# The second half of a feed-forward stage placed beside the first units of the context attention that follows it

## The chip, the cores and the metric

The kernel runs on one core of a Trainium2 chip. The metric is device time in microseconds (us) of one launch, as the median of several runs. PE is the matmul engine (TensorE), PEld its weight loads, DVE VectorE, ACT ScalarE, POOL GpSimd, and SP the engine whose queue issues nearly all DMAs here.

## The reference, cut to what matters

Two layers work on x (4 batches of 256 tokens, 256 channels) with a context of 4 batches of 4096 positions and 192 channels. Each layer is a cross attention over the context, a self-mixing attention and a feed-forward part, each added to x:

```python
x = x + _L0_xattn_ref(_layernorm(x), ctx_768, ...)
x = x + _L0_attn_ref(_layernorm(x), ...)
x = x + _L0_ffn_ref(_layernorm(x), ...)      # the stage that is moved
x = x + _L1_xattn_ref(_layernorm(x), ctx_768, ...)   # the stage it is moved beside
x = x + _L1_attn_ref(_layernorm(x), ...)
x = x + _L1_ffn_ref(_layernorm(x), ...)
```

The layer-0 feed-forward picks one of 8 experts for each token, adds the rank-4 update of that expert to the first matrix product, takes a ReLU over 1024 hidden channels, and multiplies by a second matrix:

```python
top1 = argmax(softmax(x @ gate_W.T + gate_b))
inter = relu(x @ wi_W.T + wi_b + lora[top1](x))
out = inter @ wo_W.T + wo_b
```

The layer-1 cross attention begins with scores of 4 heads of 32 channels against all 4096 positions. Only the 32 largest scores of a row are kept: `topv, topi = top_k(scores, 32)`, softmax over these, mean over the heads, then a weighted sum of context rows.

## The kernel before, in words

x stays in SBUF as 8 tiles of 128 tokens. The stages follow each other in the source (`program`, from L2040 on): layer-0 cross attention, layer-0 attention, then `l1_context_keys` (the keys of the layer-1 context attention, function `keys`, for batch 0), then `l0_ffn`, then `l1_context`, then the rest of layer 1.

`l0_ffn` (L748 to L816) normalizes all of x, turns it to channels-first (`normed_channels`, L155), works out the experts, and then runs two halves of 512 tokens. A half has 8 parts "ps_h" (L803 to L807: six matmul instructions of 512 columns on PE each, then a ReLU on ACT into `hT`) and 4 parts "ps_o" (L808 to L816: sixteen matmul instructions of 256 columns, then DVE adds the product to one tile of x, L815, and POOL adds the bias, L816). `hT` has two buffers, one for each half, and the PSUM pool of the stage has four banks.

`l1_context` (L1065) works in 32 units: 4 batches x 2 halves of the 256 tokens x 4 heads. For a unit

- `scores` (L1153) has two parts. A part is 4 mask matmuls and 4 score matmuls on PE into two PSUM tiles of two banks (pool `x1_big`, two buffers, so a part needs both), and two copies on ACT (L1175) into `sc` tiles, of which there are 8: two units.
- `best` (L1181, two parts) takes 32 MAX8 on DVE (L1187).
- `chosen` (L1189) finds the 32 largest: 4 MAX8 and 3 MATCH_REPLACE8 on DVE; POOL negates the largest (`neg`, L1198); ACT takes four exponentials of 1024 columns (L1202) into `e` tiles, of which there are 19, in a ring.
- `weighted` (L1208) cuts and weights them: four SCALAR_TENSOR_TENSOR on DVE (L1212), a reciprocal, and a diagonal matrix on POOL (L1216).

After every fourth unit, `gathered` (L1219) sums the 4 heads and multiplies by the context rows on PE (`ps_w` L1228, `ps_c` L1242, with context tiles `cx` that `load_ctx` fetches, L1143). Its steps are run one or two at a time in the following units. The loop over units (L1268) looks ahead by hand: `best(u + 1, ...)` stands around `weighted(u)`, and `scores(u + 2)` stands at the end of unit u. In units 0 to 5 of a batch the keys of the next batch are made, too (8 chunks: a DMA of 384 KB, four matmul instructions, an ACT copy, four DMAs), and its tokens are normalized and turned (`tokens`, L1109) in unit 3.

Before unit 0 stand `queries(tokens(0))`, `load_ctx(0)` (four DMAs of 768 KB and four small memsets on POOL), and the scores of units 0 and 1.

Each engine takes its instructions in a fixed order. That order is not quite the order of the source. When the program is built, a planner lists the instructions of each engine by a cost model of its own: it takes what the model has ready, and of that what stands first in the source. So in the trace the key matmuls of L1052 stand between the feed-forward's matmuls around 1535 us, although all of batch 0's keys stand ahead of the feed-forward in the source, and the layer norms of batches 1 and 2 (L95 to L99) are done around 1575 to 1592 us, although they stand in units 3 and 11. Memory comes from pools; a pool that is opened in the place of a closed one waits, tile by tile, for the last use of what lay there.

Of the kernel before, what the change touches and what calls it, by code (L numbers as in the profile page):

```python
# [11 lines left out]
F32 = mybir.dt.float32  # L12
# [7 lines left out]
PSUM = bass.MemoryType.PSUM  # L20

P = 128
B, S, D = 4, 256, 256
NB = B * 2
# [130 lines left out]
def normed_channels(c, pool, psum):  # L155

    xnT = pool.tile([P, 2, B * S], F32, tag="xnT", name="xnT")
    with c.tc.tile_pool(name="norm", bufs=1) as tmp:
        xn = tmp.tile([P, NB, D], F32, tag="xn", name="xn")
        layernorm(c, tmp, xn, c.x)  # L160
        to_channels(c, psum, xnT, xn)
    return xnT


def attn_finish(c, pool, psum, o_ps, on):
# [580 lines left out]


def l0_ffn(c, w):  # L748
    nc, tc = c.nc, c.tc
    with ExitStack() as es:  # L750
        one = es.enter_context(tc.tile_pool(name="f0_one", bufs=1))
        psum = es.enter_context(tc.tile_pool(name="f0_ps", bufs=4, space=PSUM))

        xnT = normed_channels(c, one, psum)
        two = es.enter_context(tc.tile_pool(name="f0_two", bufs=2))


# [26 lines left out]
        kept = one.tile([P, NB, 32], F32, tag="kept", name="kept")  # L784
        nc.vector.tensor_tensor(
            kept.rearrange("p n (e r) -> p (n e) r", r=4),
            low.rearrange("p n (e r) -> p (n e) r", r=4),
            hot.rearrange("p n e -> p (n e)").unsqueeze(2).to_broadcast([P, NB * 8, 4]),
            ALU.mult,
        )  # L790
        keptT = one.tile([32, B * S], F32, tag="keptT", name="keptT")
        for half in range(2):
            ps = psum.tile([P, 512], F32, tag="mm", name="ps_kt")
            for i in range(4):
                nc.tensor.transpose(ps[0:32, i * P : (i + 1) * P], kept[:, half * 4 + i, :], c.ident)
            nc.scalar.copy(keptT[:, half * 512 : (half + 1) * 512], ps[0:32, :])

        for half in range(2):
            ts = slice(half * 512, (half + 1) * 512)
            hT = two.tile([P, 8, 512], F32, tag="hT", name="hT")  # L800
            for j in range(8):
                fs = slice(j * P, (j + 1) * P)
                ps = psum.tile([P, 512], F32, tag="mm", name="ps_h")  # L803
                for k in range(2):
                    nc.tensor.matmul(ps, w.wi[:, k, fs], xnT[:, k, ts], start=(k == 0), stop=False)
                nc.tensor.matmul(ps, w.lb[:, fs], keptT[:, ts], start=False, stop=True)
                nc.scalar.activation(hT[:, j, :], ps, AF.Relu, bias=w.bi[:, j : j + 1])  # L807
# [254 lines left out]
    return w  # L1062


def l1_context(c, w, beside):  # L1065

# [11 lines left out]
    psum = w.psum  # L1078
    with ExitStack() as es:
        one = es.enter_context(tc.tile_pool(name="x1_one", bufs=1))  # L1080
        acc = es.enter_context(tc.tile_pool(name="x1_acc", bufs=1, space=PSUM))
        pst = es.enter_context(tc.tile_pool(name="x1_pt", bufs=2, space=PSUM))
        big = es.enter_context(tc.tile_pool(name="x1_big", bufs=2, space=PSUM))
        two = es.enter_context(tc.tile_pool(name="x1_two", bufs=2))
        four = es.enter_context(tc.tile_pool(name="x1_four", bufs=4))
        ews = es.enter_context(tc.tile_pool(name="x1_e", bufs=1))
        last = es.enter_context(ExitStack())
        scs = last.enter_context(tc.tile_pool(name="x1_sc", bufs=8))

        keep = one.tile([P, NB], F32, tag="keep", name="keep")  # L1090
        nc.vector.tensor_copy(keep, w.keep)
# [6 lines left out]
        places, free = [], list(tiles)  # L1098
        for u in range(len(units)):
            if u > 3:  # L1100
                g, c4 = u // 4 - 1, u % 4
# [2 lines left out]
            del free[:4]  # L1104

        def weights(u):
            return places[u]

        def tokens(b):  # L1109
# [3 lines left out]
            nc.sync.dma_start(c.xt[:, 2 * b : 2 * b + 2, :], xt)  # L1113
            xT = one.tile([P, 2, S], F32, tag="xT", name="xT")
            ps = psum.tile([P, 512], F32, tag="mm", name="ps_t")
            for k in range(2):
                for i in range(2):
                    nc.tensor.transpose(
                        ps[:, k * S + i * P : k * S + (i + 1) * P], xt[:, i, k * P : (k + 1) * P], c.ident
                    )  # L1120
            nc.vector.tensor_copy(xT.rearrange("p k n -> p (k n)"), ps)
            return xT
# [96 lines left out]
        def gathered(b, tt, es, ps_c, first, last):  # L1219

            n = 0
            for c4 in range(4):
                wTs = []
                for half in range(2):
                    ps = pst.tile([P, 512], F32, tag="pt", name="ps_w")
                    for i in range(4):
                        for h, (e, diag) in enumerate(es):
# [7 lines left out]
                    wT = two.tile([P, 512], F32, tag="wT", name="wT")  # L1235
                    nc.scalar.copy(wT, ps)  # L1236
                    wTs.append(wT)
                yield
# [11 lines left out]
                yield  # L1250
            if not last:
                return
            o = two.tile([P, DC], F32, tag="o", name="o")
# [12 lines left out]
        group, late, more = [], iter(()), iter(())  # L1266
# [1 line left out]
        for u, (b, tt, h) in enumerate(units):  # L1268
# [41 lines left out]
        last.close()  # L1310
        beside()
        for _ in late:
            pass
# [726 lines left out]
def program(tc, a, out):  # L2040
# [3 lines left out]
    with ExitStack() as es:  # L2044
# [17 lines left out]
        with tc.tile_pool(name="w_a0", bufs=1) as pool_a0:  # L2062
            pool_x0 = es.enter_context(ExitStack())
            w = l0_xattn_weights(c, pool_x0.enter_context(tc.tile_pool(name="w_x0", bufs=1, side="right")))
            pool_f0 = es.enter_context(ExitStack())
            pools, w_s4, w_f0 = [], Ctx(), Ctx()

# [8 lines left out]
            def sums(psum, last):  # L2076
# [3 lines left out]
                        pass  # L2080
                yield from s4d_sums(c, pools[0], w_s4, psum)
                pool_x0.close()
                l0_ffn_weights(c, pool_f0.enter_context(tc.tile_pool(name="w_f0", bufs=1, side="right")), w_f0)

            l0_xattn(c, w, powers)
# [2 lines left out]
        with ExitStack() as stack:  # L2088
            w = l1_context_keys(c, stack)
            for _ in w.keys(0):  # L2090
                pass
            l0_ffn(c, w_f0)
            pool_f0.close()
            w_s1 = []

            def first():
                pool = es.enter_context(tc.tile_pool(name="w_s1a", bufs=1, side="right"))
# [128 lines left out]
```

## Time and profile before

| what | value |
|---|---|
| median of 3 runs (lowest, highest) | 2508.36 us (2495.72, 2518.99) |
| the profiled execution: time, span | 2526.01 us, 2524.2 us |
| feed-forward, ps_h of the first half to its last ps_o | 1502.5 to 1550.6 us |
| feed-forward, second half | 1550.6 to 1588.4 us |
| context attention up to `chosen` of unit 0 | 1588.4 to 1604.3 us |
| units 0, 1, 2, 3 and 4 (from `neg` to the next `neg`) | 13.96, 13.60, 13.51, 13.52, 17.80 us |
| units 0 to 31 | 1604.3 to 2112 us |

The stretches are read from the timeline: the first and the last instruction of each group, and the starts of `neg` (L1198), which stands at the same place in each unit. The profiled execution took 17.65 us more than the median of the runs, so differences are worked out inside it and then set against the median. A line of the windows view gives, for a stretch of the span: its length, the busy time and the instructions of PE, PEld, DVE, ACT and POOL, the mean PE clock that was granted (1.00 is full), the share of the DMA engines' time that was used, and GB/s.

### The profile page before, as it was taken

To read this page: it belongs to the slowest core of one execution; us is meant where nothing else is said; L and a number is where in the kernel's file an instruction comes from. 1 tells how busy PE (TensorE), PEld (TensorE's weight loads), DVE (VectorE), ACT (ScalarE), POOL (GpSimd) and SP (SyncE) were. 2 spreads that over 40 slices of the span, in tenths; PEclk is the share of its full clock that TensorE was granted. 3 is DMA by queue.
4 is the path that set the end of the run, shared out by engine and by line. 5 is a ranking of instruction groups with operands and counts; after the bars stand their busy time and mean duration, and the time that the engine had idled before them with its cause. 6 is when DMAs were issued, how large, how long until landed. Compare 5 with 4: busy or idle time off the path is not lost. (4 is left out here: it accounts for less than half of the span.)

```text
span 2524.2 us, 54839 instructions
## 1 busy us (share of the span) xinstructions
PE 2379.7 (94%) x22737; PEld 1473.4 (58%) x22737; DVE 1657.5 (66%) x4026; ACT 1068.6 (42%) x1896; POOL 134.5 (5%) x208
## 2 busy tenths in 40 slices
PE   6999999999999999999999989898999999899896
PEld 4655555555555555555555544467776789456554
DVE  6666666666666666666944440898989893577554
ACT  1255555555555554556311221565656553111221
POOL 3000000000000000000000000000000010242000
PEclk7899999999999999999989999789999999798877
DMA  8221312122221222200100011310404011300110
GB/s 214 85 65 48 77 52 66 49 69 57 60 67 52 65 61 57 62 15 2 39 1 5 1 50 51 90 53 17 119 23 115 7 52 56 105 0 17 34 26 9
DMA packets 64848, 132.25 MB, mean 52 GB/s; under 512 B 12000, under 2 KB 38752, under 8 KB 64272
## 3 DMA queue, kind: packets, MB, share of 16 engines
q1 hardware_dynamic: 63088, 124.62, 17.8%
q8 instruction: 180, 2.95, 0.5%
q10 hardware_dynamic: 992, 3.02, 0.4%
q0 software_dynamic: 512, 1.05, 0.2%
q14 instruction: 76, 0.62, 0.1%
HBM read 98.14 MB, written 5.34 MB: 41 GB/s over the span
## 5 line engine op out<-in xcount | busy, mean ns | idle before, releaser
L504 DVE TENSOR_REDUCE mx<-ps_a 128x1 f32<-128x512 f32 x1024 | 659.4, 685 | 222.8 <-PE ps_a L489 219.1
L500 ACT ACTIVATE e<-ps_s 128x512 f32<-128x512 f32 x1024 | 555.8, 594 | 418.1 <-PE ps_a L489 397.8
L489 PE MATMUL ps_a<-kt,qa 32*128 32x512 f32 x2048 | 658.8, 647 | 12.2 <-DVE mx L504 9.0
L475 PE MATMUL ps_s<-qb,kt 32*128 32x256 f32 x4096 | 592.4, 401 | 0.0
L475 PEld LDWEIGHTS ps_s<-qb,kt 32*128 32x128 f32 x4096 | 349.4, 184 | 197.5 <-issue 106.7
L417 PE MATMUL o_ps<-e,v 128*32 128x256 f32 x4096 | 327.6, 391 | 0.0
L489 PEld LDWEIGHTS ps_a<-kt,qa 32*128 32x128 f32 x2048 | 231.2, 185 | 41.2 <-DVE mx L504 19.6
L1228 PEld LDWEIGHTS ps_w<-diag,e 128*128 128x128 f32 x2048 | 235.6, 194 | 24.9 <-issue 24.9
L1228 PE MATMUL ps_w<-diag,e 128*128 128x128 f32 x2048 | 241.9, 279 | 0.0
L417 PEld LDWEIGHTS o_ps<-e,v 128*32 128x32 f32 x4096 | 81.0, 108 | 246.5 <-issue 235.0
L1187 DVE MAX8 cand<-sc 128x8 f32<-128x128 f32 x1024 | 207.2, 277 | 19.5 <-ACT sc L1175 19.5
L1202 ACT ACTIVATE e<-sc,neg 128x1024 f32<-128x1024 f32 x128 | 140.7, 1143 | 119.4 <-POOL neg L1198 88.7
L1212 DVE SCALAR_TENSOR_TENSOR e<-sc,top,e 128x1024 f32<-128x1024 f32 x128 | 158.9, 1276 | 19.7 <-ACT e L1202 16.7
L1175 ACT COPY sc<-ps_s 128x1024 f32<-128x1024 f32 x128 | 123.7, 1013 | 48.7 <-PE ps_s L1166 47.4
L321 PE MATMUL ps_k<-ctxT,x_wk 32*128 32x256 f32 x1536 | 105.1, 404 | 11.6 <-DMA ctxT<-in_ctx 11.6
L1242 PEld LDWEIGHTS ps_c<-cx,wT 128*128 128x128 f32 x576 | 98.8, 196 | 21.4 <-ACT wT L1236 9.7
L1242 PE MATMUL ps_c<-cx,wT 128*128 128x193 f32 x576 | 106.4, 338 | 3.7 <-ACT wT L1236 3.7
L343 PEld LDWEIGHTS ps_v<-x_wv,ctxT 32*128 32x128 f32 x3072 | 97.5, 190 | 15.4 <-DVE mx L504 9.4
L343 PE MATMUL ps_v<-x_wv,ctxT 32*128 32x128 f32 x3072 | 104.7, 279 | 0.7
L321 PEld LDWEIGHTS ps_k<-ctxT,x_wk 32*128 32x128 f32 x1536 | 89.5, 197 | 26.4 <-issue 17.3
L1166 PE MATMUL ps_s<-kt,q 32*128 32x512 f32 x512 | 90.4, 683 | 0.0
L1052 PE MATMUL ps_k<-ctx,x_wku 96*128 96x512 f32 x128 | 71.9, 687 | 19.5 <-DMA ctx<-in_ctx 17.4
(400 smaller groups left out, 2444.9 us busy)
## 6 DMA issues: line engine op xcount, KB each, us to landing
ctxT<-in_ctx SPq DMA_DIRECT2D x62, 768.0 KB
kt<-ks SPq DMA_DIRECT2D x352, 64.0 KB
ctx<-in_ctx SPq DMA_DIRECT2D x32, 384.0 KB
cx<-in_ctx SPq DMA_DIRECT2D x16, 768.0 KB
x_w<-in_x_w SPq DMA_DIRECT2D x2, 1024.0 KB
qk<-rot SPq DMA_DIRECT2D x8, 256.0 KB
a_qk<-qk SPq DMA_DIRECT2D x16, 128.0 KB
ctxT<-in_ctx ACTq DMA_DIRECT2D x2, 768.0 KB
```

What stands on the lines that cost most here:

```text
L321: nc.tensor.matmul(ps[:, :256], w.wk[hs, gp, k, :], ctxT[hs, k, :], start=(k == 0), stop=(k == 5))
L343: nc.tensor.matmul(ps[:, ks], ctxT[hs, k, ks], w.wv[hs, gp, k, :], start=(k == 0), stop=(k == 5))
L417: nc.tensor.matmul(o_pss[u][32 * h : 32 * h + 32, :S], vs[g // 2][:, c0 : c0 + 32], ew[h][:, n % 2, :], start=(n == 0), stop=(n == GT - 1),)
L475: nc.tensor.matmul(ps[:, k * S : (k + 1) * S], kts[u % 4 // 2][hs, u % 2, ks], qbs[u][hs, :], start=True, stop=True,)
L489: nc.tensor.matmul(ps, qas[u][hs, tt * P : (tt + 1) * P], kts[u % 4 // 2][hs, u % 2, ch * 512 : (ch + 1) * 512], start=True, stop=True,)
L500: nc.scalar.activation(e, ps.rearrange("p (k n) -> p k n", k=2), AF.Exp)
L504: nc.vector.tensor_reduce(mxs[u][:, tt, h, ch : ch + 1], ps, AX.X, ALU.max)
L1187: nc.vector.max(cands[u][:, n, :], sc[u][c4][:, i // 4, (i % 4) * P : (i % 4 + 1) * P])
L1202: nc.scalar.activation(t, src, AF.Exp, bias=neg)
L1212: nc.vector.scalar_tensor_tensor(t, src, top[:, 31:32], t, ALU.is_ge, ALU.mult)
L1228: nc.tensor.matmul(ps[:, i * P : (i + 1) * P], e[c4][:, half, i * P : (i + 1) * P], diag, start=(h == 0), stop=(h == len(es) - 1),)
L1242: nc.tensor.matmul(ps_c[:, : DC + 1], wT[:, i * P : (i + 1) * P], cxs[b][t][:, j, :], start=(first and n == 0), stop=(last and n == 31),)
```

## The change

`l0_ffn` becomes a generator that stops after pairs of its first half's ps_o parts, and after each part of its second half. `l1_context` is handed that generator and runs one step of it at each place written `next(ffn)`: four times around the preparation of batch 0, after each of the four score parts of units 0 and 1, and after each score part in the loop's units 0, 1 and 2. The first step runs all up to x's tiles 0 and 1, the second finishes the first half, the third to the tenth are the second half's ps_h parts, and the last four its ps_o parts.

What goes with it, since both stages are now in memory together: `hT` has one buffer for both halves and lends its first part to the normalized x; the feed-forward's PSUM pool has three banks in place of four; the `sc` tiles lie in a pool opened earlier, on the side of the weights; 12 of the 19 `e` tiles are there from the start, and the other 7, the `cx` tiles, `wT`, `o` and the PSUM of `gathered` are opened after the feed-forward's last step, in unit 2. `load_ctx(0)` moves there too. `tokens` is split into `normed` and `turned`. `norm` as a pool of its own goes.

```diff
 def l0_ffn(c, w):
...
-        psum = es.enter_context(tc.tile_pool(name="f0_ps", bufs=4, space=PSUM))
-        xnT = normed_channels(c, one, psum)
-        two = es.enter_context(tc.tile_pool(name="f0_two", bufs=2))
+        psum = es.enter_context(tc.tile_pool(name="f0_ps", bufs=3, space=PSUM))
+        hT = one.tile([P, 8, 512], F32, tag="hT", name="hT")
+        xn = hT[:, 0:4, :].rearrange("p a (b d) -> p (a b) d", d=D)
+        layernorm(c, one, xn, c.x)
+        xnT = one.tile([P, 2, B * S], F32, tag="xnT", name="xnT")
+        to_channels(c, psum, xnT, xn)
...
         for half in range(2):
-            hT = two.tile([P, 8, 512], F32, tag="hT", name="hT")
             for j in range(8):
...
                 nc.scalar.activation(hT[:, j, :], ps, AF.Relu, bias=w.bi[:, j : j + 1])
+                if half == 1:
+                    yield
             for i in range(4):
...
                 nc.gpsimd.tensor_tensor(xi, xi, w.bo, ALU.add)
+                if half == 1 or i % 2 == 1:
+                    yield

-def l1_context(c, w, beside):
+def l1_context(c, w, scs, ffn, beside):
...
-        tiles = [ews.tile([P, 2, 512], F32, tag=f"e{i}", name=f"e{i}") for i in range(19)]
+        tiles = [ews.tile([P, 2, 512], F32, tag=f"e{i}", name=f"e{i}") for i in range(12)]
...
-        qs[0] = queries(tokens(0))
-        load_ctx(0)
+        next(ffn)
+        xt = normed(0)
+        next(ffn)
+        xT = turned(xt)
+        next(ffn)
+        qs[0] = queries(xT)
+        next(ffn)
         for u in range(2):
             for _ in scores(u):
-                pass
+                next(ffn)
...
             ahead = scores(u + 2) if u + 2 < n else iter(())
             next(ahead, None)
             next(late, None)
+            if u < 3:
+                next(ffn)
             next(ahead, None)
+            if u < 3:
+                next(ffn)
+            if u == 2:
+                for _ in ffn:
+                    pass
+                acc = es.enter_context(tc.tile_pool(name="x1_acc", bufs=1, space=PSUM))
+                pst = es.enter_context(tc.tile_pool(name="x1_pt", bufs=2, space=PSUM))
+                late_two = es.enter_context(tc.tile_pool(name="x1_late", bufs=2))
+                four = es.enter_context(tc.tile_pool(name="x1_four", bufs=4))
+                ews = es.enter_context(tc.tile_pool(name="x1_e2", bufs=1))
+                load_ctx(0)
+                tiles += [ews.tile([P, 2, 512], F32, tag=f"e{i}", name=f"e{i}") for i in range(12, 19)]
             if b + 1 < B:
...
                 if u % 8 == 3:
-                    xT = tokens(b + 1)
+                    xT = turned(normed(b + 1))
...
 def program(tc, a, out):
...
-            l0_ffn(c, w_f0)
-            pool_f0.close()
...
+            def ffn():
+                yield from l0_ffn(c, w_f0)
+                pool_f0.close()
...
-            l1_context(c, w, first)
+            l1_context(c, w, w_f0.scs, ffn(), first)
```

More of the change, by code (lines that the diff above doesn't have):

```diff
@@ L152, in to_channels @@
                 nc.vector.tensor_copy(dst, ps[:, : m * P])
[L155 to L162, printed above, removed]
 def attn_finish(c, pool, psum, o_ps, on):
@@ L1080, in l1_context @@
         one = es.enter_context(tc.tile_pool(name="x1_one", bufs=1))
-        acc = es.enter_context(tc.tile_pool(name="x1_acc", bufs=1, space=PSUM))
-        pst = es.enter_context(tc.tile_pool(name="x1_pt", bufs=2, space=PSUM))
         big = es.enter_context(tc.tile_pool(name="x1_big", bufs=2, space=PSUM))
         two = es.enter_context(tc.tile_pool(name="x1_two", bufs=2))
-        four = es.enter_context(tc.tile_pool(name="x1_four", bufs=4))
         ews = es.enter_context(tc.tile_pool(name="x1_e", bufs=1))
-        last = es.enter_context(ExitStack())
-        scs = last.enter_context(tc.tile_pool(name="x1_sc", bufs=8))
         keep = one.tile([P, NB], F32, tag="keep", name="keep")
@@ L1094, in l1_context @@
         off = one.tile([P, NB], F32, tag="off", name="off")
-        tiles = [ews.tile([P, 2, 512], F32, tag=f"e{i}", name=f"e{i}") for i in range(19)]
-        places, free = [], list(tiles)
+        tiles = [ews.tile([P, 2, 512], F32, tag=f"e{i}", name=f"e{i}") for i in range(12)]
+        places, free = [], list(range(19))
         for u in range(len(units)):
@@ L1106, in weights, with normed @@
         def weights(u):
-            return places[u]
-        def tokens(b):
+            return [tiles[i] for i in places[u]]
+        def normed(b):
             xt = one.tile([P, 2, D], F32, tag="xt", name="xt")
@@ L1113, in tokens, with turned @@
             nc.sync.dma_start(c.xt[:, 2 * b : 2 * b + 2, :], xt)
+            return xt
+        def turned(xt):
             xT = one.tile([P, 2, S], F32, tag="xT", name="xT")
@@ L1234, in gathered @@
                             )
-                    wT = two.tile([P, 512], F32, tag="wT", name="wT")
+                    wT = late_two.tile([P, 512], F32, tag="wT", name="wT")
                     nc.scalar.copy(wT, ps)
@@ L1252, in gathered @@
                 return
-            o = two.tile([P, DC], F32, tag="o", name="o")
+            o = late_two.tile([P, DC], F32, tag="o", name="o")
             nc.scalar.copy(o, ps_c[:, :DC])
@@ L1308, in l1_context @@
                 if u % 8 == 3:
-                    xT = tokens(b + 1)
-        last.close()
+                    xT = turned(normed(b + 1))
         beside()
@@ L2064, in program @@
             w = l0_xattn_weights(c, pool_x0.enter_context(tc.tile_pool(name="w_x0", bufs=1, side="right")))
+            pool_sc = es.enter_context(ExitStack())
             pool_f0 = es.enter_context(ExitStack())
@@ L2082, in sums @@
                 pool_x0.close()
+                w_f0.scs = pool_sc.enter_context(tc.tile_pool(name="x1_sc", bufs=8, side="right"))
                 l0_ffn_weights(c, pool_f0.enter_context(tc.tile_pool(name="w_f0", bufs=1, side="right")), w_f0)
@@ L2091, in program @@
                 pass
-            l0_ffn(c, w_f0)
-            pool_f0.close()
             w_s1 = []
+            def ffn():
+                yield from l0_ffn(c, w_f0)
+                pool_f0.close()
             def first():
+                pool_sc.close()
                 pool = es.enter_context(tc.tile_pool(name="w_s1a", bufs=1, side="right"))
                 w_s1.append(l1_ssm_first(c, pool))
-            l1_context(c, w, first)
+            l1_context(c, w, w_f0.scs, ffn(), first)
         l1_context_again(c)
```

## The prediction

> **What bounds the kernel now.** The page's first part comes first: PE is busy for 94% of the span, DVE for 66%.
>
> ```profile
> PE 2379.7 (94%) x22737; PEld 1473.4 (58%) x22737; DVE 1657.5 (66%) x4026; ACT 1068.6 (42%) x1896; POOL 134.5 (5%) x208
> ```
>
> That is a mean over stages. The chain of work that ended last holds only the last stages and says nothing here, so I cut the place of the change into stretches (windows view).
>
> ```profile
> core 0: us, PE busy (x) PEld busy (x) DVE busy (x) ACT busy (x) POOL busy (x), PEclk, DMA share, GB/s
> 1550.60:1588.40 37.80, 37.80 (x115) 20.09 (x115) 7.46 (x29) 5.90 (x10) 2.91 (x4) 1.00 0.02 7
> 1588.40:1594.80 6.40, 4.91 (x26) 3.41 (x25) 4.37 (x15) 0.20 (x1) 0.95 (x5) 1.00 0.81 235
> 1594.80:1604.30 9.50, 7.47 (x33) 2.79 (x33) 7.07 (x33) 3.99 (x5) 0.00 (x0) 0.68 0.67 203
> 1604.30:1618.30 14.00, 11.03 (x40) 3.78 (x37) 13.90 (x49) 11.47 (x14) 0.69 (x2) 0.62 0.00 0
> 1618.30:1631.80 13.50, 10.75 (x33) 3.91 (x32) 13.50 (x48) 11.31 (x14) 0.66 (x2) 0.61 0.32 94
> 1631.80:1645.40 13.60, 10.32 (x32) 3.11 (x32) 13.60 (x49) 8.64 (x11) 0.66 (x2) 0.64 0.35 93
> 1645.40:1658.60 13.20, 11.37 (x37) 5.95 (x36) 13.20 (x47) 7.93 (x11) 0.66 (x2) 0.63 0.22 59
> 1658.60:1676.70 18.10, 17.95 (x115) 14.82 (x115) 14.61 (x51) 9.86 (x13) 0.66 (x2) 0.88 0.13 38
> 1676.70:1745.00 68.30, 61.59 (x448) 49.03 (x447) 59.94 (x203) 39.54 (x52) 4.72 (x8) 0.95 0.09 25
> 1745.00:2112.00 367.00, 344.08 (x2497) 275.48 (x2495) 327.63 (x1061) 222.17 (x296) 30.44 (x57) 0.97 0.20 57
> ```
>
> The second half of the feed-forward (first row) is PE alone: 37.80 of 37.80 us at full clock, DVE 7.46. In units 0 to 3 (1604.3 to 1658.6) it is the other way round: DVE is busy for all of each unit, and PE, though it looks 80% busy, runs at a clock of 0.61 to 0.64. Busy time by clock gives its work at full clock: 5.08, 6.84, 6.56, 6.60 and 7.16 us in the five rows from 1594.8, 32.2 us in 63.8. From unit 4 on the gather fills PE again (17.95 of 18.10, then 94% of the last row): there both engines are near full, and what PE has not done by 1658.6 is late.
>
> The timeline of PE gives the start of the attention, and the waits say what ends PE's idle time there.
>
> ```profile
> 1588.38 0.60 PE L1118 MATMUL ps_t<-ident,xt 128*128 128x128 f32 x4
> 1589.77 1.99 PE L1131 MATMUL ps_q<-xT,x_wq 128*128 128x256 f32 x8 [0.31 <-DVE xT L1121]
> 1592.87 1.99 PE L1131 MATMUL ps_q<-xT,x_wq 128*128 128x256 f32 x8 [1.11 <-DVE q L1138]
> 1594.79 1.14 PE L1166 MATMUL ps_s<-kt,q 32*128 32x512 f32 x8
> 1597.11 0.39 PE L1163 MATMUL ps_s<-mask,pick 32*128 32x512 bf16 x2 [1.18 <-ACT sc L1175]
> ```
>
> ```profile
> PE ps_s L1163 <- ACT sc L1175: 15.4, 21, 1.6
> PE ps_k L1052 <- DMA ctx<-in_ctx: 9.8, 8, 2.4
> ```
>
> **The change, part by part.** All sums are against the profiled execution, 2526.0 us, which lies 17.6 above the median of the runs.
>
> *1. The stretch of PE alone goes:* -37.8 us (first row; 8 ps_h parts of 2.96 and 4 ps_o parts of 3.45 make it up).
>
> *2. The start.* From the last ps_o to the first score, 6.4 us: transposes 0.60, queries 2 x 1.99, the other 1.83 waiting. Now two ps_h parts (5.92) stand among these and can use the 1.83: 6.4 + 5.92 - 1.83 = 10.5, so +4.1. Bounds: 0, if the planner lists them behind, +5.9, if no wait is used. The layer norm of batch 0 needs x's tiles 0 and 1, final at 1545.4; the same chain took 2.84 us before (1575.45 to 1578.29), so it ends near 1548.3, under the ps_o of tiles 2 and 3, which run to 1550.6; without that cover it would cost 2.84. First score: 1594.8 - 33.7 = 1561.1.
>
> *3. PE until the gather.* 31.9 us of feed-forward (37.8 - 5.92) meet 32.2 of other work: 64.1 in a room of 63.8. At full clock that is +0.3. The mixed rows from 1658.6 have clocks of 0.88, 0.95 and 0.97: +9.0, +3.7, +2.3. I take 0.95, the first row with several kinds of matmul and steady load: +3.7; low end +0.3, high end +9.0.
>
> The row of 0.62 would give another sum, and here a page bears on it. The Trainium skill, TensorE: Matmul & The Clock Gate, section "A second HAM failure mode: psum-queue depth-cycling", says that a stream that cycles through PSUM banks idles for moments often enough for the clock to swing between half and full, and that speaks against filling gaps between score parts. By it, at a mean of 0.75, PE would need an estimated 85 us and the gain would be an estimated 11 us. The stretches at 1.00 hold dense matmuls, the ones at 0.62 score parts alone; no row of this trace has both in one stretch.
>
> *4. DVE, ACT and POOL until the gather.* (a) One ps_h part stands between unit 0's two score parts: second part at +1.3 + 2.96 from the first, its copy 2.4 later, so the second half of MAX8 starts at +6.9 in place of +6.3 (1601.1): +0.6, bounds -1 and +3. (b) Some four ReLUs (0.69 each) fall into unit 0, whose ACT is busy 11.47 of 14.00: 14.2, so +0.2, bounds 0 and 2.75. (c) Four DVE additions of 0.42 move from an idle DVE into full units: +1.7 (0 if an idle moment takes them). (d) Batch 2's layer norm, done at 1590 to 1592 for free, must wait for tiles 4 and 5 in unit 1. Batch 3's, which already fell among the units (its table load stands at 1685.43), made its unit 0.3 us longer (14.98 us from `neg` to `neg`, 14.68 for the unit before): +0.3; at most its DVE work of 2.8 and two table loads of 1.28, 5.4. (e) DVE's addition and POOL's bias for a tile wait for its ps_o; behind them stand DVE's MAX8, POOL's four memsets and `neg` of the next unit, and behind `neg` the exponentials and then the SCALAR_TENSOR_TENSOR. If PE is late, these wait: 0 to one ps_o part, 3.45; I take +1. Unit 3's `e` tiles lie in memory that the last ps_o frees and wait for the same event. Sum +3.8.
>
> The gather needs both PE and the `e` tiles, so of 3 (+3.7) and 4 (+3.8) the later counts: +3.8.
>
> *5. DMA.* `load_ctx(0)` moves from 1588.6 to the end of the last ps_o, about 53 us after the first score, 1614. Its four issues took SP 5.64 us, its 3 MB some 16 us (shares 0.81 and 0.67). The first reader, ps_c, ran at 1669.1 and comes near 1639: hidden by 9 us. But SP's queue holds the loads and stores of batch 1's keys behind it, and these now share the engines with it; PE waited 2.4 us at most for such a load (waits, above). One half of that, +1.0; bounds 0 and two such waits, 4.8. The keys are needed from unit 6 on. *6. Three PSUM banks for four:* one copy of 0.68 may be waited for at the start, +0.3 (0 to 0.7). `hT` with one buffer costs nothing: a ReLU writes after a ps_h part which PE runs after the last ps_o that reads it. *7.* `sc` on the other side: the loads that follow waited for its last use at 2112.5 before, and still do. Units 4 to 31 have no fixed times in them, so the shift passes through.
>
> Sum: -37.8 + 4.1 + 3.8 + 1.0 + 0.3 = -28.6 us: 2497.4 for the profiled execution, 2508.4 - 28.6 = 2480 for the median. All good ends: -37.8 + 0.3 = -37.5 (2471). All bad ends of 2, 4, 5 and 6: -37.8 + 5.9 + 16.3 (3 + 2.75 + 1.7 + 5.4 + 3.45) + 5.5 = -10.1 (2498).
>
> **The rivals.** *A. DVE stalls on a late PE* (no faster by more than 20 us). The lists are fixed; if they place the four additions earlier than PE comes, each costs DVE up to 3.45 us and the lag does not shrink, and the swinging exponentials add theirs: four times 3.45 in place of the 1.0 of 4e, 12.8 more, gives -15.8: 2493. For it: DVE has no idle time in units 1 to 3. Against: PE's lag by sum 3 is under 4 us in all. *B. Slower: PE stays at the clock of units 0 to 3.* Place: 1561 to the gather. At 0.62 the 64.1 us take 103.4, a lag of 39.6 in place of 3.8, so +7.2 and 2516; it decides against the change from the point where the lag is 33.7 - 1.3 = 32.4, a clock of 0.67. For it: the four rows of 0.61 to 0.64 come from score parts that stay. Against: with PE never idle the rows show 0.88 and more. *C. It doesn't do what it says:* the planner lists the parts as a block ahead of the scores; then the start is as before and only memory changes: 0 to -4, 2506.
>
> **How the numbers follow.** The forecast (gains of 20 to 37.5) has 0.62, A 0.20, B 0.12, C 0.06. About 1%, 25 us, is what a measurement of this kernel can tell from no change. Three in four of the forecast's cases gain more: faster 0.47. The rest of it (0.15), most of A (0.18), C and a third of B are within 1%: 0.43. Slower: 0.10. The range has the best end less the scatter of the runs (2496 to 2519, about 11 either way), 2460, and reaches over A and C to 2512; the forecast's own range is 2465 to 2492.
>
> **What would show it.** Right: ps_h and ps_o stand between the score parts; first score near 1561; PE's clock above 0.9 from there to the gather; units 0 to 3 still 13.5 to 15 us; gather near 1630; the same distances from there to the end. Wrong: units 1 to 3 above 16 us with DVE idle before L815 or L1212 (A); clocks near 0.6 with ps_h at 5 us a part (B); a second half in one block (C); waits of PE for `ctx` above 5 us.

## The result and the profile after

| | before | after |
|---|---|---|
| median of 17 runs each, taken together (lowest, highest) | 2504.72 us (2486.51, 2527.22) | 2483.44 us (2464.97, 2496.51) |
| profiled execution: time, span | 2526.01, 2524.2 us | 2496.51, 2494.7 us |

The ratio is 0.9919, with a 95% interval of 0.9898 to 0.9940: 20 us less, between 15 and 26, or 0.8%. 2480 us were predicted, a gain of 28.6; the chance that the text gave for a gain under 1% was 0.43.

The first part of the page has changed little (the lines here answer to those shown of before):

```profile
PE 2352.6 (94%) x22737; PEld 1465.7 (59%) x22737; DVE 1663.7 (67%) x4026; ACT 1070.7 (43%) x1898; POOL 135.0 (5%) x208
```

The windows view of the kernel after, cut at the first score and close to the start of `chosen` in units 0 to 6, some 0.5 us ahead of each `neg` (columns as before: length, then busy time of PE, PEld, DVE, ACT, POOL, then the granted PE clock, the DMA share, GB/s):

```profile
core 0: us, PE busy (x) PEld busy (x) DVE busy (x) ACT busy (x) POOL busy (x), PEclk, DMA share, GB/s
1560.50:1571.00 10.50, 10.50 (x48) 4.31 (x48) 6.50 (x33) 6.68 (x8) 0.00 (x0) 1.00 0.00 1
1571.00:1585.50 14.50, 12.59 (x39) 4.63 (x38) 14.17 (x47) 9.98 (x13) 0.69 (x2) 0.76 0.00 0
1585.50:1600.30 14.80, 11.24 (x34) 3.78 (x36) 14.35 (x49) 9.58 (x12) 0.66 (x2) 0.77 0.00 1
1600.30:1615.90 15.60, 12.47 (x66) 7.67 (x58) 15.22 (x51) 10.28 (x13) 1.39 (x3) 1.00 0.19 49
1615.90:1630.90 15.00, 12.96 (x54) 8.05 (x54) 11.76 (x55) 6.51 (x10) 2.11 (x4) 1.00 0.31 84
1630.90:1650.90 20.00, 16.76 (x113) 13.20 (x112) 19.37 (x53) 14.47 (x18) 1.61 (x7) 0.91 0.77 219
1650.90:1672.20 21.30, 19.44 (x116) 14.40 (x120) 17.53 (x60) 13.22 (x17) 0.67 (x2) 0.92 0.23 68
```

The stretch of PE alone has gone, and PE still has 1.9 to 3.6 us of idle time in each of units 0 to 3. DVE has almost none in units 0 to 2 (14.17 of 14.50, 14.35 of 14.80, 15.22 of 15.60). The units are longer than the 13.5 us that DVE needed before. So the second column to read is DVE's, not PE's.

The timeline of PE in the kernel after:

```profile
1551.65 0.60 PE L1116 MATMUL ps_t<-ident,xt 128*128 128x128 f32 x4
1552.09 1.88 PE L799 MATMUL ps_h<-xnT,f_wi 128*128 128x512 f32 x4
...
1560.52 0.71 PE L1164 MATMUL ps_s<-kt,q 32*128 32x512 f32 x3
...
1635.93 8.37 PE L1226 MATMUL ps_w<-diag,e 128*128 128x128 f32 x58 [2.32 <-DVE e L1210]
```

The feed-forward stands where it was written, the first score comes at 1560.5 in place of 1594.8, and the first long run of the gather (`ps_w`) at 1635.9 in place of 1658.6. Of the 34.3 us of lead at the first score, 22.6 are left there. The waits of PE over the whole span:

```profile
PE ps_s L1161 <- ACT sc L1173: 14.7, 19, 2.2
...
PE ps_k L1050 <- DMA ctx<-in_ctx: 10.9, 9, 2.4
```

The starts of `neg` on POOL give the place of the loss. The lead of after over before, unit by unit from unit 0 to unit 7, is 33.4, 32.8, 31.6, 29.4, 28.0, 25.8, 19.2 and 19.5 us. From there on it stays: 19.3 at unit 8, 19.1 at the last unit. So the units end 19 us sooner, which fits the 20 us of the many runs. The rest of the 29.5 us between the two profiled spans arises behind the last unit, in stages whose code is the same.

The start brought what was hoped, and units 0 to 5 gave 14 us of it back. Units 0 to 6 last 102.05 us in before and 115.95 in after. In that stretch DVE is busy for 98.16 us before and 106.70 after, and idle for 3.9 and 9.3: 8.5 us more work and 5.4 us more idle time. The groups of DVE in that stretch name two parts of the work:

- the four additions of the feed-forward: 1.6 us;
- the statistics and small steps of batch 2's layer norm, which were done ahead of the units before: 2.6 us.

The remaining 4.3 us are in no new instruction. The order of DVE's list, which the timeline shows, fits them. Unit 1 of the kernel before, from the first of the seven dependent steps that find the 32 largest to the last:

```profile
1618.33 0.42 DVE L1195 MAX8 top<-cand 128x8 f32<-128x256 f32 x1
1618.65 0.28 DVE L1187 MAX8 cand<-sc 128x8 f32<-128x128 f32 x1
...
1618.90 0.41 DVE L1200 MATCH_REPLACE8 cand<-top,cand 128x256 f32<-128x256 f32 x1
1619.23 0.29 DVE L1187 MAX8 cand<-sc 128x8 f32<-128x128 f32 x1
1619.43 0.41 DVE L1195 MAX8 top<-cand 128x8 f32<-128x256 f32 x1
...
1621.97 1.83 DVE L1187 MAX8 cand<-sc 128x8 f32<-128x128 f32 x9
```

The same steps of unit 1 in the kernel after:

```profile
1585.54 0.43 DVE L1193 MAX8 top<-cand 128x8 f32<-128x256 f32 x1
1586.01 0.09 DVE L1198 MATCH_VALUE_LOAD cand<-top,cand 128x8 f32 x1
1586.09 0.41 DVE L1198 MATCH_REPLACE8 cand<-top,cand 128x256 f32<-128x256 f32 x1
1586.53 0.43 DVE L1193 MAX8 top<-cand 128x8 f32<-128x256 f32 x1
...
1589.03 1.28 DVE L1210 SCALAR_TENSOR_TENSOR e<-sc,top,e 128x1024 f32<-128x1024 f32 x1
```

Before, six MAX8 of unit 2 stand between the seven steps, and all of it takes 3.64 us. After, the seven steps stand bare, and take 3.49. Six MAX8 in a row of their own take 1.16 us (16 take 3.10 from start to start), so the bare order loses 1.0 us per unit. In the kernel before, four MAX8 stand between the steps of unit 0 and six in each of units 1 to 5; in the kernel after there are none, though additions and layer-norm steps fill a few of the gaps in units 3 and 4. In unit 0 it costs 0.6. At 1.0 us for six, the 34 of before are worth 5.7 us; the 4.3 us of busy time is what is left when the new instructions are taken off, not a count of its own.

The kernel before loses this filling too, only later: from unit 6 to unit 31 no MAX8 stands between its steps. Its units 8 to 14, which do for the next batch what units 0 to 6 do for the first and have the gather of the batch before beside them, take 108.3 us, with DVE busy for 101.6. By this comparison some 6 of the 13.9 us bring the first batch to what the other batches take in both kernels, and the rest lies above that.

The idle time has two main sources, in ACT's timeline and in POOL's (kernel after):

```profile
1615.01 1.28 ACT L77 ACT_TABLE_LOAD   x1
...
1633.41 1.15 ACT L1200 ACTIVATE e<-sc,neg 128x1024 f32<-128x1024 f32 x1 [5.66 <-POOL x L812]
...
1663.53 1.28 ACT L77 ACT_TABLE_LOAD   x1
...
1665.05 1.28 ACT L1200 ACT_TABLE_LOAD   x1
1666.34 1.15 ACT L1200 ACTIVATE e<-sc,neg 128x1024 f32<-128x1024 f32 x1
```

```profile
1616.50 0.21 POOL L1196 TENSOR_SCALAR neg<-top 128x1 f32<-128x1 f32 x1 [3.71 <-DVE top L1193]
...
1632.65 0.73 POOL L812 TENSOR_TENSOR x<-x,f_bo 128x256 f32<-128x256 f32 x1 [0.27 <-DVE x L811]
```

The exponentials of unit 3 can run from 1616.5, when `neg` is there, but start at 1633.4, 16.9 us later, right behind the feed-forward's last bias, whose memory their `e` tiles take. The last ps_o ends at 1629.4, but DVE's addition of it stands behind steps of unit 4, at 1632.2. And the square root of batch 2's layer norm now falls among the exponentials, as that of batch 3 did before, each with two table loads, one ahead of the root and one ahead of the next exponential. DVE's waits from unit 0 to unit 6:

```profile
DVE e L1210 <- ACT e L1200: 1.9, 3, 1.5
DVE rs_y L79 <- ACT rs_r L77: 1.5, 1, 1.5
DVE ln_st L95 <- POOL x L812: 1.3, 2, 0.8
```

### The profile page after: what moved, and what is told of

Read it like the earlier page. It is cut to its first block, busy times and chain, and to the rows that moved or that the text cites. A ratio compares the mean times of both kernels' runs of the same rounds, so it can differ in the third digit from the quotient of the medians.

```text
span 2494.7 us, 54822 instructions
## 1 busy us (share of the span) xinstructions
PE 2352.6 (94%) x22737; PEld 1465.7 (59%) x22737; DVE 1663.7 (67%) x4026; ACT 1070.7 (43%) x1898; POOL 135.0 (5%) x208
## 5 line engine op out<-in xcount | busy, mean ns | idle before, releaser
L479 PEld LDWEIGHTS ps_a<-kt,qa 32*128 32x128 f32 x2048 | 231.1, 185 | 41.3 <-DVE mx L494 19.6
L311 PEld LDWEIGHTS ps_k<-ctxT,x_wk 32*128 32x128 f32 x1536 | 89.0, 196 | 28.6 <-issue 18.5
L812 POOL TENSOR_TENSOR x<-x,f_bo 128x256 f32<-128x256 f32 x8 | 5.8, 727 | 1511.1 <-DVE x L811 1511.1
L1164 PE MATMUL ps_s<-kt,q 32*128 32x512 f32 x512 | 81.8, 640 | 0.0
```

What stands on the lines that cost most here:

```text
L311: nc.tensor.matmul(ps[:, :256], w.wk[hs, gp, k, :], ctxT[hs, k, :], start=(k == 0), stop=(k == 5))
L479: nc.tensor.matmul(ps, qas[u][hs, tt * P : (tt + 1) * P], kts[u % 4 // 2][hs, u % 2, ch * 512 : (ch + 1) * 512], start=True, stop=True,)
```

## The experiments

Whole times scatter by 0.3% and more, so each kernel is judged by the length of its units, from `neg` to `neg`, in its profile. Where two kernels have the same list for a unit, these agree within 0.02 us (units 0 and 1 in many rows of the table). Unit 7 is left out, since at the batch's end it took 20.8 to 23.7 us in one and the same code. DVE's columns are for units 0 to 6.

| kernel | time or ratio to before | u0 | u1 | u2 | u3 | u4 | u5 | u0-6 | DVE busy | DVE idle |
|---|---|---|---|---|---|---|---|---|---|---|
| before | 1 | 13.96 | 13.60 | 13.51 | 13.52 | 17.80 | 14.68 | 102.05 | 98.16 | 3.89 |
| after | 0.9919 | 14.54 | 14.79 | 15.65 | 14.95 | 20.03 | 21.27 | 115.95 | 106.70 | 9.25 |
| e1_newton | 2485.4 us | 14.53 | 14.79 | 15.64 | 14.24 | 20.02 | 19.47 | 113.41 | 108.36 | 5.05 |
| e2_ffn_first | 2491.7 us | 14.53 | 14.79 | 18.49 | 21.18 | 13.44 | 20.07 | 117.25 | 106.71 | 10.54 |
| e3_light | 2491.5 us | 14.53 | 14.80 | 15.51 | 16.84 | 18.56 | 23.70 | 118.68 | 105.57 | 13.11 |
| e4_block | 2509.0 us | 13.86 | 13.60 | 13.51 | 13.52 | 16.65 | 14.69 | 100.81 | 98.07 | 2.74 |
| e6_pool_first | 2492.5 us | 14.53 | 14.80 | 15.65 | 14.94 | 19.31 | 25.26 | 119.23 | 106.64 | 12.59 |
| e7_sooner | 2478.6 us | 14.54 | 14.79 | 19.63 | 15.29 | 17.27 | 20.07 | 116.33 | 106.61 | 9.72 |
| e7n | 2491.4 us | 14.53 | 14.79 | 20.70 | 15.24 | 18.84 | 19.56 | 118.42 | 108.58 | 9.84 |
| e8n | 2505.5 us | 14.55 | 16.48 | 18.47 | 15.25 | 17.03 | 19.67 | 116.21 | 108.31 | 7.90 |
| e9_order | 0.9927 [0.9894, 0.9960] | 14.53 | 17.34 | 17.10 | 14.93 | 21.86 | 24.50 | 124.98 | 103.97 | 21.01 |
| e9n | 0.9952 [0.9924, 0.9981] | 14.53 | 17.33 | 17.11 | 13.77 | 21.86 | 23.72 | 123.50 | 104.76 | 18.74 |
| e10_lead | 0.9949 [0.9923, 0.9976] | 13.85 | 13.60 | 15.45 | 24.67 | 20.03 | 20.03 | 122.35 | 106.16 | 16.19 |
| e10n | 0.9920 [0.9893, 0.9947] | 13.84 | 13.60 | 14.72 | 23.46 | 20.02 | 19.48 | 119.85 | 107.72 | 12.13 |

A time in us is a single execution; the kernel before took 2524.7 us beside the four of e1 to e4, and 2503.8 beside the four of e6 to e8. Edits are against the kernel after.

**e1_newton: no table loads among the exponentials.**

```diff
...
-            layernorm(c, one, xt, c.x[:, 2 * b : 2 * b + 2, :], n=2)
+            layernorm(c, one, xt, c.x[:, 2 * b : 2 * b + 2, :], n=2, root=newton_rsqrt if b > 1 else rsqrt)
```

> The layer norms of batches 2 and 3 take their reciprocal root on DVE alone (Newton steps), so no square root stands among ACT's exponentials. Measure: units 0 to 7, from the first neg to the neg of unit 8, 139.6 us with the change and 125.6 before. If the two pairs of table loads (2 x 2 x 1.28 us, with ACT waiting in between for DVE) make a good part of the 14 us lost there, units 3 and 5 become shorter, 5 us together, and the stretch comes to about 135. If the loss is PE that is late or DMA, the stretch stays at 139 to 140.5 (the Newton steps add about 1 us of DVE for each batch).

Units 3 and 5 lose 0.7 and 1.8 us, 2.5 in all, and nothing else moves. DVE does 1.7 us more (the Newton steps) and idles 4.2 less. So the square roots cost at least 2.5 us here, and most of DVE's new idle time goes with them.

**e2_ffn_first: the feed-forward's part ahead of each score part in the loop.**

```diff
             ahead = scores(u + 2) if u + 2 < n else iter(())
+            if u < 3:
+                next(ffn)
             next(ahead, None)
             next(late, None)
...
                 next(ffn)
             next(ahead, None)
-            if u < 3:
-                next(ffn)
             if u == 2:
```

> In units 0 to 2 each feed-forward part stands ahead of the score part, not behind it, so that PE has work while a score part waits for ACT to free its PSUM (8.2 us of such waits from the first score to unit 7). If PE that is late at the gather makes the loss, the last ps_o ends some 6 us earlier and units 0 to 7 come to 134 to 136 us in place of 139.6. If the loss is in ACT's table loads or in the late context load, they stay at 138 to 140.

The loss moves from units 4 and 5 to units 2 and 3, and is 1.3 us larger in sum. The order of the two within a slot is not the cause.

**e3_light: less work for PE.** Each ps_o part of the second half has two matmul instructions in place of sixteen; DVE, POOL and ACT do the same as in the kernel after. The output lacks seven of the eight products for these tokens.

```diff
-                for j in range(8):
+                for j in range(8 if half == 0 else 1):
...
-                        ps[:, :D], hT[:, j, i * P : (i + 1) * P], w.wo[:, j, :], start=(j == 0), stop=(j == 7)
+                        ps[:, :D], hT[:, j, i * P : (i + 1) * P], w.wo[:, j, :], start=(j == 0), stop=(half == 1 or j == 7)
```

> The second half's four ps_o parts take one of their eight products only (the output leaves out the other seven for those tokens), so 12 us of PE work less in units 1 to 3, with DVE's and POOL's additions, the layer norms behind them and the context load all where they are. If PE that is late makes the loss, units 0 to 7 fall to about 129 us. If it is table loads and additions, they stay above 137.

12 us less of PE work bring nothing: units 0 to 6 take 118.7 us. PE's busy time in them falls by 4 us only (96.2 for 100.2), while the granted clock is lower (0.78 and 0.70 in units 2 and 3, where it was 1.00); but PE is idle for 22.5 us in place of 15.7, and the last ps_o ends 56.2 us behind unit 0's `neg` in place of 57.9. So the feed-forward's end hardly moves with PE's load, and a PE that comes late by its load is not what costs the 14 us.

**e4_block: the feed-forward ahead of the attention, all else as after** (the smaller PSUM pool, the memory order, the late place of `load_ctx` in the source).

```diff
-        next(ffn)
+        for _ in ffn:
+            pass
         xt = normed(0)
-        next(ffn)
         xT = turned(xt)
...
         for u in range(2):
             for _ in scores(u):
-                next(ffn)
+                pass
...
```

> The feed-forward runs to its end ahead of the attention, as before; the pools, the late context load and the late e tiles of the change stay. If only the interleaving counts, units 0 to 7 take about 126 us and the whole about as long as before (2505, within 5). If the new memory order or the late context load is what costs units 4 and 5 their time, units 0 to 7 take 132 us or more and the whole is over 2510.

The units are those of before, or better (100.81 us). So the new places in memory and the three PSUM banks cost nothing by themselves. The late context loads and late `e` tiles were to be tested too, but are not: with the feed-forward ended ahead of the units, the loads went out at 1587.6, as in before (1588.6). What costs is that the parts stand beside the units, or what comes late with them.

**e6_pool_first: other addresses for unit 3's `e` tiles.**

```diff
+                ews = es.enter_context(tc.tile_pool(name="x1_e2", bufs=1))
                 late_two = es.enter_context(tc.tile_pool(name="x1_late", bufs=2))
                 four = es.enter_context(tc.tile_pool(name="x1_four", bufs=4))
-                ews = es.enter_context(tc.tile_pool(name="x1_e2", bufs=1))
```

> One thing is changed against the kernel after: the pool of unit 3's `e` tiles is opened ahead of the other two late pools, so that these tiles get other addresses. Theory M (memory): unit 3's exponentials start 16.9 us after their `neg` because their tiles lie in memory that the last bias addition of the feed-forward on POOL frees; at an address that is freed by an earlier reader, they start 3 us sooner or more (before 1630.5 on the profile's clock) and units 4 and 5, which take 20.0 and 21.3 us now, together lose 3 us or more. Rival S (switches): the loss is in the two table loads around each square root; then the first exponential of unit 3 may move, but units 0 to 6 stay at 116 us (within 1). Rival D (DVE is full): whatever DVE doesn't do in unit 3 it does in unit 4; units 0 to 6 stay at 116 too, with a shorter idle time of DVE in no place.

The exponentials start at 1628.9, 4 us sooner against their `neg`, and unit 4 is 0.7 shorter; but unit 5 is 4 longer. The wait has moved to PE, as its waits from 1640 to 1676 show:

```profile
PE ps_k L1050 <- DMA ctx<-in_ctx: 8.2, 2, 7.2
```

`load_ctx(0)`, with its 3 MB, went out at 1632.8 in place of 1629.5 (4 us later, counted from unit 0's `neg`), and the loads for batch 1's keys stood behind it in SP's queue. The expectation of theory M (3 us off units 4 and 5) missed.

**e7_sooner, e7n, e8n: the feed-forward ends a unit sooner.** In e7_sooner the two slots of units 0 and 1 take two parts and one; e7n adds the Newton root; e8n puts two parts behind each of the two score parts of unit 1, ahead of the loop (which its expectation counts as unit 1's slots), has one in each slot of units 0 and 1, and has the Newton root. The edit of e7_sooner:

```diff
-            if u < 3:
+            if u < 2:
+                next(ffn)
                 next(ffn)
             next(ahead, None)
-            if u < 3:
+            if u < 2:
                 next(ffn)
-            if u == 2:
+            if u == 1:
```

> The feed-forward's parts are spread over units 0 and 1 in place of 0 to 2 (two parts, then one, in each slot), and the late pools are opened one unit sooner. Theory M: the last bias addition comes before unit 3's `neg` (by about 1620), its exponentials follow `neg` within 3 us, and units 3 to 5 come to 47 us (13.5 + 18 + 15) in place of 56.3; units 0 to 2 get longer, by at most the PE work that they take on, some 4 us; units 0 to 6 come to 109 us, 5 to 7 less than after. Rival L (PE is late): the same PE work in two units makes these longer by as much as units 4 and 5 gain; units 0 to 6 stay at 115 to 118 us. Rival S: no gain but what the places of the table loads give, 2.5 us at most.

> As the run before, and with the layer norm of batches 2 and 3 by the Newton root on DVE, so that no table load falls among the exponentials. Theory M with the 2.5 us that the Newton root alone gave: units 0 to 6 at 106 to 107 us, the same last stages, 9 us under after. Rival L: 113 us, what the Newton root gave alone.

> As e7n, but the extra parts stand in unit 1 alone: one part in each slot of unit 0, two in each of unit 1's. It tells where PE has room. Theory M: the same 106 to 108 us for units 0 to 6, since the last bias addition comes at about the same time (about 1622, before unit 3's `neg`). Rival L: unit 1 gets longer than 18 us, and the sum stays at 113.

In e7_sooner the exponentials of unit 3 start here, 1.95 us after their `neg` (1610.82):

```profile
1612.77 1.15 ACT L1200 ACTIVATE e<-sc,neg 128x1024 f32<-128x1024 f32 x1 [4.42 <-POOL x L812]
```

Unit 4 comes back to 17.3 us, as in before (17.0 in e8n, 18.8 in e7n), so most of its 2.2 us goes with the late exponentials. But in e7_sooner unit 2, where three additions and the layer norm now meet, takes 19.6, and the sums of the three are about the same as after's: 116.3, 118.4 and 116.2 us. Theory M is right on the place and wrong on the gain. What stays the same in all of these is the last columns: DVE is busy for 104 to 109 us in every kernel with the parts beside the units, and for 98 in the two without.

**e9_order, e9n: the old order of DVE's list, by force.** In units 1 to 5, six MAX8 of the next unit are put between the dependent steps; e9n has the Newton root as well.

```diff
...
+        def chosen(u, fill):
+
+            def step(op, *args):
+                if step.n and fill:
+                    ins = best(u + 1, [step.n - 1])
+                    with tc.issue_after(getattr(ins, "ins", ins)):
+                        op(*args)
...
-                nc.vector.max(t8, flat)
+                step(nc.vector.max, t8, flat)
...
-                    nc.vector.match_replace(flat, t8, flat, TAKEN)
+                    step(nc.vector.match_replace, flat, t8, flat, TAKEN)
```

> Only the order of DVE's list is changed against the kernel after: in units 1 to 5 the first six MAX8 of the next unit are put between the seven dependent steps that find the 32 largest, as they stand in the list of the kernel before. Theory O (order): these steps bare take 3.50 us, with six MAX8 among them 3.64 us, though six MAX8 by themselves take 1.17 us; so the bare order loses 1.0 us in each such unit. Units 1 and 2 come to 13.8 and 14.6 us (14.8 and 15.65 after), units 3 to 5 give another 1 or 2, and units 0 to 6 come to 112 to 113 us (115.95 after). Rival G (given back): units 4 and 5 end when PE and the exponentials end, so that what units 1 and 2 gain is waited for there: units 0 to 6 stay within 1 us of 116. Rival N: the order costs nothing since the steps are held by something else; units 1 and 2 stay at 14.8 and 15.6.

> The same order of DVE's list, and the Newton root for the layer norms of batches 2 and 3. If the two causes add, units 0 to 6 come to 109 to 111 us, 5 to 7 under after, and the time is some 0.25% under that of after (ratio to before 0.989). If the order is given back in units 4 and 5, 113 us as with the Newton root alone.

DVE's busy time falls by 2.7 us, as the filled gaps should make it, but its idle time grows by 11.8. All three theories named there missed. DVE's waits of e9_order, units 0 to 6:

```profile
DVE cand L1185 <- ACT sc L1173: 11.6, 4, 5.1
```

The next unit's scores are not there yet. Their copies stand on ACT among the exponentials of the present unit. So the bare order is not a whim of the planner: it follows from scores that come later.

**e10_lead, e10n: the four score parts of units 0 and 1 together,** the four ps_h parts from between them in the slots of units 0 and 1; e10n with the Newton root.

```diff
             for _ in scores(u):
-                next(ffn)
+                pass
...
-            if u < 3:
+            for _ in range((2, 2, 1)[u] if u < 3 else 0):
                 next(ffn)
```

> The four score parts of units 0 and 1 stand together, without feed-forward parts between them; the four parts that stood there go to units 0 and 1, two in each slot. All else is as in the kernel after. Theory H (head start): in the kernel before, the scores are one whole unit ahead, so MAX8 of the next unit can fill the gaps between the seven dependent steps; in the kernel after they are half a unit behind that, and DVE has no slack to win it back. With the head start kept, units 0 and 1 come to 13.9 and 13.7 us (14.5 and 14.8 after) as before; from unit 2 on, two feed-forward parts between score parts use the head start up again, the bare order returns, and units 2 to 6 give back a part: units 0 to 6 at 113 to 115 us (115.95 after). Rival P: PE's feed-forward work itself has to be paid in units 0 to 3 wherever it stands; units 0 to 6 at 116 to 118. Rival F: the order has nothing to do with the head start; units 0 and 1 stay at 14.5 us or more.

> As the run before, with the Newton root for the layer norms of batches 2 and 3. If the causes add, units 0 to 6 come to 110 to 113 us and the ratio to the kernel before is 0.988 to 0.990; if PE's work has to be paid anyway, units 0 to 6 at 113 to 116 and the ratio 0.990 to 0.992, as after.

Units 0 and 1 take 13.85 and 13.60 us, those of before to 0.1 us, with the MAX8 back between the steps. Theory H holds for these units: what lengthened them was that the scores lost their head start of half a unit when ps_h parts were put between the first four score parts. The head start is then used up later, and at a higher price: unit 3 takes 24.7 us. In ACT's timeline of e10_lead:

```profile
1626.40 1.01 ACT L1173 COPY sc<-ps_s 128x1024 f32<-128x1024 f32 x1 [5.01 <-PE ps_s L1164]
...
1639.72 1.15 ACT L1200 ACTIVATE e<-sc,neg 128x1024 f32<-128x1024 f32 x1 [1.89 <-POOL x L812]
```

The feed-forward ends only at 1639, and unit 3's exponentials wait for it again, for longer. No version is shown to beat the kernel after: e10n has the same ratio (0.9920 [0.9893, 0.9947]), e7_sooner's single time of 2478.6 comes with units of the same length as after's, and the 2.5 us that e1_newton's units gain are too few for its single time to show.

## Why the prediction was right, and where not

The time, the range and the mechanism came out right: 2483 against 2480, and a PE-only stretch turned into work beside a DVE-bound one. That the two times lie so close is partly luck: over 17 runs the median of before is 2504.72, 3.6 us under the 2508.36 from which the prediction counted. The gain was 20 us in place of 28.6, the lower edge of the forecast's own cases and nearer to rival A's 15.8 than to 28.6, and the missing part has one place, step 4. Of the signs of being right, the place of the parts and the first score held; the clock above 0.9 did not in units 0 and 1, unit 2 took 15.65 us where 15 was the most, and the gather began at 1635.9 in place of 1630.

*Steps 1 and 2* held. The first score came at 1560.5 (1561.1 predicted), and unit 0's `neg` 33.4 us sooner.

*Step 3* named PE as one of two engines that could set the gather's start, with +3.7. PE was not it (e3_light). The clock was 1.00 in the stretches with ps_o parts, and 0.76 and 0.77 in units 0 and 1, between the two values weighed; but there PE was idle for 1.9 and 3.6 us and DVE was full, so the lower clock cost nothing: in e1_newton unit 0 has a clock of 0.88 and takes 14.53 us, after 14.54. What the Trainium skill says (TensorE: Matmul & The Clock Gate, "A second HAM failure mode: psum-queue depth-cycling") agrees with these two rows and not with the two after them. The estimate of an 11 us gain drawn from it took PE for the limit, and fell with that. Rival B fell for the same reason.

*Step 4* was mis-sized: +3.8 taken; measured were 0.9 up to unit 0's `neg` and 13.9 over units 0 to 6, 14.8 in all, within the sum of its bad ends (16.3).

- *4a* (+0.6) was counted once, for the way from the first score to unit 0's `neg`, and that took 11.0 us in place of 10.1 (its second half of MAX8 started at +7.1; the text has +6.9, though its own 1.3, 2.96 and 2.4 make 6.7). But a DVE without slack does not win the delay back: from then on the scores are half a unit late, the next unit's MAX8 no longer fill the gaps of the dependent steps, and it costs another 0.6 in unit 0 and up to 1.0 in each unit to unit 5, 4.3 in all by the difference of DVE's busy times. The prediction had no term for work that DVE did for nothing because other work filled its gaps. e10_lead shows the cause for units 0 and 1; for the later ones it is read from the timelines.
- *4b* (+0.2) can't be told apart.
- *4c* was right: 1.6 measured, 1.7 taken.
- *4d* took +0.3, from batch 3's layer norm among units that PE bounded. In units that DVE bounds, batch 2's 2.6 us of DVE work come on top, and two more table loads. The bound of 5.4 was probably the better value; no run took the layer norm's DVE work away. e1_newton gives 2.5 us for the roots of both batches.
- *4e* took +1 and saw the wait: unit 3's `e` tiles "wait for the same event". They waited for it 16.9 us. The date was wrong: step 5 has the last ps_o at 1614, 53 us after the first score, and it ended at 1629.4. The four ps_o parts start at 1600.9, 1608.9, 1620.9 and 1625.7, with score parts and key products between them; no run took apart which of these holds them. The wait put the four SCALAR_TENSOR_TENSOR of unit 3 into unit 4, left DVE 3.2 us idle in unit 3, and delayed the gather. The 2.2 us of unit 4 go when the exponentials come sooner (e7_sooner, e8n; e7n keeps 1.0 of them); earlier ends cost as much elsewhere.

*Step 5* (+1.0, though half of 2.4 is 1.2): PE's waits for `ctx` went from 3.1 to 3.8 us in units 0 to 6 and from 9.8 to 10.9 us in the whole span, the longest is 2.4 still. The size fits, though no run has the late loads without the parts, and e6_pool_first shows how near its bad end was: 4 us later, and one wait was 7.2. *Steps 6 and 7*: nothing to be seen, and e4_block has both at no cost.

*Rival A* had the right engine and the wrong event: DVE waits for no ps_o in the kernel after; it does more, and waits for ACT and POOL. *Rival C* is out by the timeline.

What stays open: unit 5 takes 19.5 us or more in every version with the parts beside the units, and 14.7 in the two without. Its last exponential waits for the gather's second run there (2.3 us in e7n), as it does in unit 13 of before; units 13 and 21 take 19.5 us in both kernels. In unit 5 of before that run starts 3.0 us ahead of `neg` (1674.24 against 1677.26); in unit 5 of after it starts 5.9 us behind it (1657.42 against 1651.48), as in unit 13 of before (1810.42 against 1804.48). So unit 5 has taken on the order of the other batches; no run put the old one back. Nor was a version tried that takes the four additions and batch 2's layer norm off DVE in these units, which the DVE column suggests.

## What to carry to other kernels

When work is moved beside a stage, ask first which engine that stage has no slack on, and count for this engine every instruction that comes along, also those that were free in the old place; a layer norm or an addition that was hidden before can be paid in full there. Look in the timeline for independent instructions that fill the gaps of a dependent chain: they come at almost no cost, and are lost when their input comes half a step later. In a stage without slack a delay put in at the start is not caught up, so count what it costs in each step that follows, up to the step where the old kernel had lost its lead as well (here unit 6), not once.

## What the runs showed of the hardware

- Seven dependent DVE steps took 3.49 us bare and 3.64 us with six independent MAX8 between them: 0.025 us for each MAX8, against 0.19 in a row.
- A table load took 1.28 us and the exponential behind it started at once (load at 1665.05, exponential at 1666.34). The Trainium skill (ScalarE: Activation LUTs, "What ACT_TABLE_LOAD costs") adds some 1.38 us of draining to the same 1.28 for each switch. The timeline shows no such gap here; what the loads cost beyond their own time was DVE's waits for the work behind them (1.51 us for batch 3's root, 0.96 us for the exponential behind batch 2's second load).
- Units that DVE fills took the same time at different granted PE clocks: unit 0 took 13.85 us at 0.50 (e10_lead) and 13.84 at 0.75 (e10n), with DVE busy for 13.8.
- The unit at a batch's end took 20.8 to 23.7 us between executions and between batches of one execution, while most others repeated to 0.05 us (14.71 to 14.75).
